# Query projection of the second batch by seven products instead of eight, in a fused cross-attention kernel

## The chip, the cores and the metric

The kernel runs on one core of a Trainium2 chip, in float32. The metric is the device time of one execution in microseconds. The kernel before takes 497.75 us (median of 3 runs, 497.58 to 497.92).

## The reference

Two batches of 2048 tokens (640 channels, 20 heads of 32) attend to 154 context rows, the first 77 and the last 77 each with a softmax of its own; both results are added, projected and added to the input.

```python
text, ip = ctx[:, :77], ctx[:, 77:]
q = split_heads(x @ Wq.T)                                   # (2, 20, 2048, 32)
out = attend(q, split_heads(text @ Wk.T), split_heads(text @ Wv.T)) \
    + attend(q, split_heads(ip @ Wk_ip.T), split_heads(ip @ Wv_ip.T))   # softmax(q k / sqrt(32)) v
return merge_heads(out) @ Wo.T + bo + x
```

## The kernel before

All matrices lie with the contracted dimension on the 128 partitions. The 640 channels are five chunks of 128, each four heads. One chunk of one batch is a step `q` (0 to 9, five for each batch); a step has two units `u` of 1024 tokens, and a unit has two blocks `h` of 512. For a block, `queries` (L198, matmul in L201) projects one chunk of queries: five matmuls of 128x128 weights by 512 tokens into one PSUM bank. `take_queries` (L209) reads the bank on ACT, scales it and puts it in one of five buffers `qT`. `scores` (L226, matmul in L233) multiplies 32-row heads by the keys. Then a group of the unit (three groups: 3, 3 and 2 tiles of 128 tokens; 24, 24 and 16 rows of heads) goes through the softmax: ACT copies the scores into `pb` (K, L245), DVE takes the maxima (M, L281 or L284), POOL subtracts them (S, L295), ACT takes exponentials (E, L301 or L269), DVE sums (D, L306) and inverts (I, L311), POOL normalises (N, L316), DVE transposes in 32x32 squares (T, L323). Groups in the table `DIRECT` skip K and S and read the bank; those in `BIASED` skip S and give the maxima to ACT as bias; in `SUMMED` ACT also makes the sums. When all six groups of a step are transposed, `attend` (L325, matmul in L332) multiplies by the values with 16 tiles of 32x32 in the array at a time, and ACT copies the result into `aT`. The projections of the keys and values (L142) and the output projection of the first batch (seven products for eight, L483 to L521, and L471 for the last chunk) fill PE between these. The second batch's output projection (L848, sums in L792 and L794) comes at the end.

A float32 matmul shows as two passes on PE in the profile: L201 has 200 matmuls and 400 passes.

The tokens lie in four resident blocks `xs` of 128x5x512 (1.28 MB). The first batch's four blocks are loaded once. For the second batch the blocks are loaded again for each unit and block, 20 times, into three of the places in turn (`place_of`, L179; `load_block`, L183); the fourth place holds sums of the output projection. The values are spread by small copies on SP's queue (`spread_v`, L154: eight for half a step).

The order of everything is the list `SCHEDULE`, a text that a planner wrote: `emit` (L632) goes through its words, and each engine does its instructions in that order. In a word the letter is the step, then come its numbers, and behind "@" the PSUM bank or half: `R0.10@1` are the scores of group 0 of unit 10, `q.10.0@3` the queries of unit 10, block 0, and `cq.10.0` their reading, `A.3@1` the attention of step 3, `m6.0` product 6 of the output projection, `LX` a load of a token block, `LQ` of query weights, `LO` of the output weights, `VS` a spread of values, `SF` and `SS` loads and stores of the output sums.

## Time and profile before

| | |
|---|---|
| median of 3 runs | 497.75 us |
| span of the profiled execution, first to last instruction | 496.7 us |
| PE busy | 490.3 us (99%) |
| DVE busy | 408.5 us (82%) |
| POOL busy | 362.5 us (73%) |
| ACT busy | 315.0 us (63%) |
| DMA, read and written | 54.94 and 10.49 MB, 132 GB/s over the span |

The profile is of one execution; its own time is its span of 496.7 us and about 1.0 us around it, by the median of the runs. Times are in microseconds unless marked ns. A row of the groups has the line, the engine, the operation, what it writes and reads, the shape, the count; then the busy time of all and the mean duration of one in ns; then the idle time of the engine just before them, and what ended it. PE's matmuls overlap each other, so the mean duration of one is longer than the distance from one to the next; the chain of waits, in order of time, gives that distance. PEld is the loading of weights, beside PE.

### The profile page before, as it was taken

The page shows a single profiled execution, that of the slowest core. Times are in us where ns is not written, and L with a number is a line of the kernel's source. Part 1 is how long each engine was busy: PE and PEld are TensorE (multiplying, and loading weights), DVE is VectorE, ACT ScalarE, POOL GpSimd, SP SyncE. Part 2 cuts the span into 40 slices and gives each one's busy share as a digit, 9 for nine tenths or more (in the row PEclk, how much of TensorE's full clock was granted, in tenths as well). Part 3 has the DMA queues.
Part 4 walks back from the last instruction along what each step waited for, and adds up shares of the span by engine and source line. Part 5 has one row for each costly group of instructions (what it writes and reads, how often), then busy time and mean ns, then how long its engine had stood idle before and what let it go on. Part 6 is the DMA issues. An engine that isn't in the chain of part 4 may idle for free.

```text
span 496.7 us, 10482 instructions
## 1 busy us (share of the span) xinstructions
PE 490.3 (99%) x4114; PEld 287.9 (58%) x4114; DVE 408.5 (82%) x412; ACT 315.0 (63%) x1021; POOL 362.5 (73%) x157
## 2 busy tenths in 40 slices
PE   8999999999999999999999999999999999999997
PEld 5676657657547556456647654755755675444442
DVE  0069989979979989969976896687999978898877
ACT  1165878978978778668999786587578966100000
POOL 0069978798888999989874858565899888284830
PEclk9999999999999999999999999999999999999999
DMA  8991440332360454886445177418525401420115
GB/s 259 356 246 40 132 120 1 106 93 69 92 213 3 132 178 132 274 273 237 158 152 191 58 244 210 133 57 246 174 69 171 127 23 43 149 84 1 43 73 223
DMA packets 67474, 69.38 MB, mean 140 GB/s; under 512 B 5473, under 2 KB 47201, under 8 KB 67425
## 3 DMA queue, kind: packets, MB, share of 16 engines
q1 hardware_dynamic: 66704, 68.00, 43.8%
q8 instruction: 32, 0.52, 0.5%
q10 hardware_dynamic: 720, 0.72, 0.4%
q14 instruction: 18, 0.14, 0.1%
HBM read 54.94 MB, written 10.49 MB: 132 GB/s over the span
## 4 chain that ended last, share of the span: by engine, by line
PE 92%; DMA 3%; SPq 1%; DVE 1%; POOL 1%; ACT 1%; issue 0%; POOLq 0%
PE bank L201 33%; PE bank L848 11%; PE bank L490 10%; PE bank L233 10%; PE bank L332 10%; PE bank L142 9%; PE bank L471 6%; PE bank L500 3%; DMA aT<-in_L_xattn_Wk_ip_dram 2%; DMA wq<-in_L_xattn_Wq_dram 2%; SPq L534 1%; POOL pb L316 1%; DVE den L306 0%; ACT pb L301 0%; SPq L132 0%
## 5 line engine op out<-in xcount | busy, mean ns | idle before, releaser
L316 POOL TENSOR_TENSOR pb<-pb,rden 128x1848 f32<-128x1848 f32 (+1 forms) x60 | 176.1, 2944 | 39.7 <-DVE rden L311 35.5
L201 PE MATMUL bank<-x,wq 128*128 128x512 f32 x400 | 180.4, 601 | 0.6 <-DMA x<-in_x_dram 0.5
L295 POOL TENSOR_TENSOR pb<-pb,mx 128x1848 f32<-128x1848 f32 (+1 forms) x38 | 119.3, 3152 | 51.8 <-DVE mx L281 51.5
L201 PEld LDWEIGHTS bank<-x,wq 128*128 128x128 f32 x400 | 74.1, 191 | 86.7 <-issue 80.8
L323 DVE STREAM_TRANSPOSE pb<-pb 128x1920 f32<-128x1920 f32 (+1 forms) x60 | 115.7, 1932 | 4.9 <-POOL pb L316 4.3
L281 DVE TENSOR_REDUCE mx<-pb 128x24 f32<-128x1848 f32 (+1 forms) x51 | 93.7, 1850 | 30.7 <-ACT pb L245 30.5
L245 ACT COPY pb<-bank 128x462 f32<-128x462 f32 (+1 forms) x204 | 87.2, 539 | 36.0 <-PE bank L233 35.4
L306 DVE TENSOR_REDUCE den<-pb 128x24 f32<-128x1848 f32 (+1 forms) x47 | 88.7, 1895 | 17.6 <-ACT pb L301 13.3
L301 ACT ACTIVATE pb<-pb 128x1848 f32<-128x1848 f32 (+1 forms) x38 | 64.2, 1696 | 17.8 <-POOL pb L295 17.5
L269 ACT ACTIVATE pb<-pb,mx 128x77 f32<-128x77 f32 x224 | 67.8, 364 | 0.3 <-DVE mx L281 0.2
L233 PEld LDWEIGHTS bank<-kT,qT 32*128 32x128 f32 x1280 | 45.4, 184 | 26.9 <-issue 15.6
L269 ACT ACTIVATE pb<-bank,mx 128x77 f32<-128x77 f32 x184 | 51.8, 386 | 9.3 <-DVE mx L284 9.3
L233 PE MATMUL bank<-kT,qT 32*128 32x154 f32 x1280 | 56.2, 305 | 0.3 <-ACT kT L559 0.3
L332 PE MATMUL bank<-pb,v 32*32 32x512 f32 x1600 | 55.2, 597 | 0.0
L142 PE MATMUL bank<-wo_ct,aT 128*128 128x154 f32 x320 | 45.6, 296 | 0.3 <-DMA aT<-in_L_xattn_Wk_ip_dram 0.3
L142 PEld LDWEIGHTS bank<-wo_ct,aT 128*128 128x128 f32 x320 | 42.9, 188 | 3.6 <-issue 2.2
L332 PEld LDWEIGHTS bank<-pb,v 32*32 32x32 f32 x1600 | 29.9, 103 | 22.8 <-issue 10.7
L211 ACT ACTIVATE qT<-bank 128x512 f32<-128x512 f32 x40 | 24.2, 619 | 22.1 <-PE bank L201 22.0
L471 PE MATMUL bank<-aT,wo_ct 128*128 128x512 f32 x80 | 36.1, 596 | 0.0
L269 ACT ACTIVATION_READ_ACCUMULATOR pb<-bank,mx 128x1 f32 x128 | 33.6, 267 | 0.0
L490 PE MATMUL bank<-aT,wo_ct 128*128 128x256 f32 x128 | 32.3, 385 | 0.0
L490 PEld LDWEIGHTS bank<-aT,wo_ct 128*128 128x128 f32 x128 | 23.7, 190 | 6.5 <-issue 3.0
(75 smaller groups left out, 434.4 us busy)
## 6 DMA issues: line engine op xcount, KB each, us to landing
x<-in_x_dram SPq DMA_DIRECT2D x20, 1280.0 KB, 6.7
out_dram<-acc SPq DMA_DIRECT2D x20, 256.0 KB, 2.3
x<-in_x_dram SPq DMA_DIRECT2D x18, 256.0 KB, 5.9
acc<-in_x_dram SPq DMA_DIRECT2D x16, 256.0 KB, 4.7
out_dram<-x SPq DMA_DIRECT2D x15, 256.0 KB, 2.0
v<-vS SPq DMA_DIRECT2D x160, 20.0 KB, 2.8
wq<-in_L_xattn_Wq_dram SPq DMA_DIRECT2D x9, 320.0 KB, 5.0
aT<-in_L_xattn_Wk_dram SPq DMA_DIRECT2D x5, 512.0 KB, 5.5
```

The source lines that it names most:

```text
L142: nc.tensor.matmul(keys_in(out), loaded[n][:, k, :], cT[:, k, :, t, :], start=(k == 0), stop=(k == NCC - 1))
L201: nc.tensor.matmul(pq, wqs[q % 3][:, k, :], xs[place_of(u, h)][:, k, :], start=(k == 0), stop=(k == NC - 1),)
L233: nc.tensor.matmul(ps[g][:, ts(t, 2 * L)], qTs[(u, h)][g * D : (g + 1) * D, ts(st, P)], kT[g * D : (g + 1) * D, c, b].rearrange("p t l -> ...
L245: nc.scalar.copy(keys_of(u, s)[:, :, g], ps[g][:, : n * 2 * L].rearrange("p (n l) -> p n l", n=n))
L269: nc.scalar.activation(row, row if ps is None else rows_in(ps[g], n)[:, t, x], AF.Exp, bias=maxs[(u, s)][:, *one], accum_out=None if den i ...
L281: nc.vector.tensor_reduce(mx, rows_of(u, s), AX.X, ALU.max, negate=negate)
L295: nc.gpsimd.tensor_tensor(rows_of(u, s), rows_of(u, s), maxs[(u, s)].unsqueeze(3).to_broadcast([P, n, 2, L]), ALU.subtract)
L306: nc.vector.tensor_reduce(den_of(u, s), rows_of(u, s), AX.X, ALU.add)
L316: nc.gpsimd.tensor_tensor(rows_of(u, s), rows_of(u, s), rdens[(u, s)].unsqueeze(3).to_broadcast([P, n, 2, L]), ALU.mult)
L323: nc.vector.transpose(p, p)
L332: nc.tensor.matmul(pa[r][g * D : (g + 1) * D, :], v4s[q % 2][rows, g, k, :], zones[rows, :, g, k, :], start=(k == 0), stop=(k == NK - 1),)
L490: nc.tensor.matmul(part, w_of[m][:, kp, op], t_of(m, b, i)[:, kp], start=(op == kp == 0 and m in (1, 2, 5)), stop=(op == 1 and kp == 1 and ...
```

## The change

For four of the second batch's five chunks (steps 5 and 6 are pair 0, steps 7 and 8 are pair 1) the queries of two chunks and one block of 512 tokens are made together. The two output chunks and the two halves of 256 tokens form a 2x2 block, and so do the four first input chunks (even and odd); seven products of 2x2 matmuls with sums of tokens and of weights take the place of eight, as the output projection already does. The fifth input chunk is added by four plain matmuls. Step 9 (units 18 and 19) and the first batch keep the old projection. The words are:

- `g.p.i.m` (`q_product`): product m of pair p and token block i on PE. Products 6, 7 and 4 go on in the bank of product 1, and 3 in that of 5.
- `t.p.i.m` (`take_q_product`): products 1, 5, 6 and 4 are read by ACT into a half of a query buffer, 2, 3 and 7 are added to or taken from it by DVE.
- `U.p.i.n.e` (`sum_x`): one of four sums of tokens, on POOL, or on DVE where e is d (the eight sums n = 2).
- `Z.p.n.e` (`sum_wq`): sums of query weights, on POOL, eight instructions for each pair.

Sums 2, 3 and 4 are written over the block that they are made from, so a block serves one pair only and is then loaded anew. There are 12 loads `LX` for 20, into two places in turn for three. The third place (`xs[2]`, `SPARE`) now holds two more query buffers, the first token sum and the weight sums; before, three of the second batch's blocks were still resident for the tail and the fourth was loaded into `acc` and `res`; now two are, and the third is loaded into the spare place ahead of the fourth, in `LA` (L809). The scale 1/sqrt(32) moves from the reading of the queries to that of the keys. `DIRECT` goes from 9 to 7 groups, `BIASED` from 13 to 16, `SUMMED` from 13 to 9, and the whole list is planned anew.

```diff
-        (11, 0), (13, 0), (13, 2), (14, 0), (14, 2), (15, 1), (15, 2), (16, 2), (18, 1),
+        (3, 2), (7, 1), (11, 0), (11, 2), (13, 0), (13, 2), (15, 1),
...
+    def first_of(u):
+        q, b, c, sub = step_of(u)
+        return u - SUB if b and c % 2 else u
 
     def place_of(u, h):
         _, b, _, sub = step_of(u)
-        return late.index((u, h)) % XROOM if b else sub * NH + h
+        return late.index((first_of(u), h)) % RING if b else sub * NH + h
...
+    spare = xs[SPARE].rearrange("p k t -> p (k t)")
+    q_more = [spare[:, ts(n, TB)] for n in range(2)]
+    x_first = spare[:, ds(2 * TB, TB)].rearrange("p (k t) -> p k t", k=2)
+    wq_room = spare[:, ds(3 * TB, 8 * P)].rearrange("p (k o) -> p k o", o=P)
...
-        nc.scalar.mul(qT, pq, SCALE)
-        qTs[(u, h)] = qT
+        nc.scalar.copy(new_q(u, h), pq)
...
+    def sum_x(p, i, n, eng):
+        x, y = {
+            1: lambda: (x_part(p, i, 0, 0), x_part(p, i, 0, 1)),
+            2: lambda: (x_sum(p, i, 1), x_part(p, i, 1, 1)),
+            3: lambda: (x_part(p, i, 0, 1), x_part(p, i, 1, 1)),
+            4: lambda: (x_sum(p, i, 2), x_part(p, i, 1, 0)),
+        }[n]()
+        eng.tensor_tensor(x_sum(p, i, n), x, y, ALU.add)
...
+        part = ps[:, :HT]
+        for kp in range(2):
+            nc.tensor.matmul(
+                part, w[:, kp], x[:, kp], start=(kp == 0 and m in (1, 2, 5)), stop=(kp == 1 and not fifth),
+                skip_group_check=True,
+            )
+        if fifth:
+            w5, h = fifth()
+            five = xs[place_of(*unit_of(p, i))][:, NC - 1, ts(h, HT)]
+            nc.tensor.matmul(part, w5, five, start=False, stop=True, skip_group_check=True)
...
+        t = (qTs[(u, h)] if (u, h) in qTs else new_q(u, h))[:, ts(half, HT)]
+        if m in (2, 3, 7):
+            nc.vector.tensor_tensor(t, t, ps[:, :HT], ALU.add if m == 2 else ALU.subtract)
+        elif half:
+            nc.scalar.mul(t, ps[:, :HT], -1.0)
+        else:
+            nc.scalar.copy(t, ps[:, :HT])
...
-        "R0.0@1 R1.0@0 K0.0 q.1.0@4 LK.5 K1.0 M0.0 M1.0 S0.0 R2.0@0 v.0.0@6 K2.0 cq.1.0 S1.0 M2.0 E0.0 v.0.1@0 LK.6 "
+        "LK.5 R2.0@0 K2.0 M2.0 R0.0@1 R1.0@0 K0.0 K1.0 E2.0 M0.0 S0.0 E0.0 q.1.0@4 M1.0 S1.0 D0.0 I0.0 LK.4 q.1.1@6 "
...
+            home[third] = xs[SPARE]
+            nc.sync.dma_start(
+                out=xs[SPARE], in_=xT[:, ds(S + third * TB, TB)].rearrange("(k p) t -> p k t", p=P)
+            )
```

What the new list does to three places of the program. The first is PE a few steps ahead of the attention of step 4, where the queries of units 10 and 11 are made. Before, three groups of queries stand together between scores (the last row of one unit's scores, the groups, the first row of the next):

```order
L233 MATMUL bank_7_74<-kT_79,qT_9_1_1528 128x154
L201 MATMUL bank_0_67<-x_1_83,wq_2_77 128x512 x5
L201 MATMUL bank_2_69<-x_2_84,wq_2_77 128x512 x5
L201 MATMUL bank_3_70<-x_0_82,wq_2_77 128x512 x5
L233 MATMUL bank_4_71<-kT_79,qT_10_0_1610 128x154
```

Now products of two token blocks are mixed there (blocks 1 and 2 of pair 0; `x_1` and `x_0` are the two places, `x_2` the spare one with the sums; L617 are the two matmuls of a product, L624 the fifth chunk, L143 a value projection):

```order
L617 MATMUL bank_5_69<-x_0_79,wq_2_74 128x256 x2
L143 MATMUL bank_0_64<-wo_ct_98,aT_83 128x154 x8
L617 MATMUL bank_4_68<-x_1_80,wq_0_72 128x256 x2
L624 MATMUL bank_4_68<-x_1_80,wq_0_72 128x256
L617 MATMUL bank_3_67<-x_0_79,wq_2_74 128x256 x2
L624 MATMUL bank_3_67<-x_0_79,wq_2_74 128x256
L617 MATMUL bank_1_65<-x_1_80,x_2_81 128x256 x2
L624 MATMUL bank_1_65<-x_1_80,x_2_81 128x256
L617 MATMUL bank_5_69<-x_0_79,x_2_81 128x256 x2
```

And a little later in the same list, products 5 and 3 of block 2 on bank 7, then product 7 on bank 5, between the scores of unit 10:

```order
L259 MATMUL bank_3_67<-kT_76,x_2_81 128x154
L617 MATMUL bank_7_71<-x_2_81 128x256 x2
L624 MATMUL bank_7_71<-x_0_79,x_2_81 128x256
L617 MATMUL bank_7_71<-x_0_79,x_2_81 128x256 x2
L624 MATMUL bank_7_71<-x_0_79,x_2_81 128x256
L617 MATMUL bank_5_69<-x_0_79,wq_0_72 128x256 x2
```

Groups of five wide matmuls have become pieces of two or three narrow ones, several banks are under way at once, and product 3 of block 2 follows product 5 on its bank with nothing between.

The second place is SP's queue at the second batch's first token blocks. Before (L186 loads a token block, L158 spreads values, L132 loads key or value weights, L192 query weights, L461 a part of the output sums):

```order
L186 DMA x_1_83<-in_x_dram 128x5x512
L158 DMA v4_1_81<-vS0_1_94 32x160 x8
L186 DMA x_2_84<-in_x_dram 128x5x512
L132 DMA aT_86<-in_L0_xattn_Wv_ip_dram 128x8x128
L461 DMA acc_87<-in_x_dram 128x2x256
L158 DMA v4_1_81<-vS1_95 32x160 x8
L186 DMA x_0_82<-in_x_dram 128x5x512
```

Now (L192 is the token block, L159 the spread, L133 the weights, L220 query weights, L165 the output weights):

```order
L192 DMA x_1_80<-in_x_dram 128x5x512
L133 DMA aT_83<-in_L0_xattn_Wv_ip_dram 128x8x128
L133 DMA aT_83<-in_L0_xattn_Wv_dram 128x8x128
L159 DMA v4_1_78<-vS1_97 32x160 x8
L192 DMA x_0_79<-in_x_dram 128x5x512
L220 DMA wq_1_73<-in_L0_xattn_Wq_dram 128x5x128
L165 DMA wo_ct_98<-in_L0_xattn_Wo_dram 128x5x640
L192 DMA x_1_80<-in_x_dram 128x5x512
```

The blocks alternate between two places, the third block stands behind eight spread copies, and the fourth behind the output weights.

The third place is DVE and POOL at units 8 and 9. DVE before (L281 maxima, L306 sums, L311 inverses, L323 transposes, L152 the squares of the values):

```order
L281 TENSOR_REDUCE mx_9_0_1679<-pb_89 128x24
L152 STREAM_TRANSPOSE vS0_0_93<-vT_91 128x160
L152 STREAM_TRANSPOSE vS1_95<-vT_91 128x160
L281 TENSOR_REDUCE mx_9_2_1727<-pb_89 128x16
L281 TENSOR_REDUCE mx_9_1_1745<-pb_89 128x24
```

DVE now (L308 maxima, L333 sums, L338 inverses, L570 a token sum, L633 a take of a product):

```order
L633 TENSOR_TENSOR x_2_81<-x_2_81,bank_3_67 128x256
L333 TENSOR_REDUCE den_8_2_1727<-pb_91 128x16
L338 RECIPROCAL rden_8_2_1729<-den_8_2_1727 128x16
L308 TENSOR_REDUCE mx_9_0_1733<-pb_91 128x24
L570 TENSOR_TENSOR x_1_80<-x_2_81,x_1_80 128x2x256
L308 TENSOR_REDUCE mx_9_2_1741<-pb_91 128x16
```

POOL now, at the same place (L322 subtracts, L343 normalises, L570 a token sum):

```order
L322 TENSOR_TENSOR pb_91<-pb_91,mx_8_1_1648 128x12x154
L570 TENSOR_TENSOR x_2_81<-x_1_80 128x512
L343 TENSOR_TENSOR pb_91<-pb_91,rden_8_0_1653 128x12x154
L570 TENSOR_TENSOR x_1_80<-x_1_80 128x2x256
L322 TENSOR_TENSOR pb_91<-pb_91,mx_9_0_1733 128x12x154
L343 TENSOR_TENSOR pb_91<-pb_91,rden_8_2_1729 128x8x154
```

Takes and token sums stand between the softmax operations on both engines; DVE's token sum (sum 2 of block 1) reads what POOL's first one (sum 1) wrote, while POOL goes on with its list.

More of the change, by code (lines that the diff above doesn't have):

```diff
@@ L92 @@
     aT = const.tile([P, (NC + 1) * NHB, TB], F32, name="aT")
+    q_slots = [const.tile([P, TB], F32, name=f"qs_{n}") for n in range(QS)]
     acc = const.tile([P, NC - 1, TB], F32, name="acc")
@@ L188, in load_block, with new_q, used_q @@
         )
+    spare = xs[SPARE].rearrange("p k t -> p (k t)")
+    q_more = [spare[:, ts(n, TB)] for n in range(2)]
+    x_first = spare[:, ds(2 * TB, TB)].rearrange("p (k t) -> p k t", k=2)
+    wq_room = spare[:, ds(3 * TB, 8 * P)].rearrange("p (k o) -> p k o", o=P)
+    q_uses, q_idle, q_late = {}, list(q_slots), list(q_more)
+    def new_q(u, h):
+        if u >= NU // 2 and q_late:
+            q_idle[:0] = q_late
+            q_late.clear()
+        t = q_idle.pop(0)
+        qTs[(u, h)], q_uses[(u, h)] = t, NT // NH
+        return t
+    def used_q(u, h):
+        q_uses[(u, h)] -= 1
+        if not q_uses[(u, h)]:
+            q_idle.append(qTs[(u, h)])
     def load_wq(q):
@@ L809, in finish @@
         elif k == "LA":
-            for u, h in late[-XROOM:]:
+            for u, h in late[-RING:]:
                 home[step_of(u)[3] * NH + h] = xs[place_of(u, h)]
-            (fourth,) = set(range(NHB)) - set(home)
+            third, fourth = sorted(set(range(NHB)) - set(home))
+            home[third] = xs[SPARE]
+            nc.sync.dma_start(
+                out=xs[SPARE], in_=xT[:, ds(S + third * TB, TB)].rearrange("(k p) t -> p k t", p=P)
+            )
             nc.sync.dma_start(
```

71 lines of the change are left out of this document (63 added, 8 removed), and 131 rows, old and new, of the table SCHEDULE.

## The prediction

> **What bounds the kernel now.** I read the page first: who is busy, and what the last chain is made of.
>
> ```profile
> span 496.7 us, 10482 instructions
> PE 490.3 (99%) x4114; PEld 287.9 (58%) x4114; DVE 408.5 (82%) x412; ACT 315.0 (63%) x1021; POOL 362.5 (73%) x157
> PE 92%; DMA 3%; SPq 1%; DVE 1%; POOL 1%; ACT 1%; issue 0%; POOLq 0%
> L201 PE MATMUL bank<-x,wq 128*128 128x512 f32 x400 | 180.4, 601 | 0.6 <-DMA x<-in_x_dram 0.5
> ```
>
> PE is busy 99% of the span, and 92% of the last chain is PE. The costliest group is the projection of the queries (L201): 400 passes, two for each of its 200 matmuls. So an edit is worth what it takes off PE's own row, less any wait that it opens there. "Busy" need not mean well spaced, so I then read the chain of waits in order of time, between 180 and 262 us.
>
> ```profile
> 224.07 0.86 PE bank L490 x4
> ...
> 225.36 4.29 PE bank L471 x10
> ...
> 234.19 0.74 PE bank L233 x16
> 234.92 4.49 PE bank L201 x10
> 239.41 1.00 PE bank L233 x24
> ```
>
> This gives the prices. A 512-column pass follows the last one after 429 ns (4.29 for 10), a 256-column pass after 215 ns (0.86 for 4). The scores (L233) work on 32 rows: 8 more of their passes cost 0.26 (1.00 less 0.74), so 16 are worth 0.52, and a visit costs 0.22 beyond its work. The ten passes between two such visits cost 0.20 more than ten that follow other 128-row work (4.49 against 4.29). A visit to 32-row work thus costs 0.42 us in turns.
>
> Who could take PE's place? I read the windows for the two fullest stretches between attentions.
>
> ```profile
> 211.60:254.60 43.00, 42.92 (x386) 24.80 (x382) 39.04 (x35) 36.69 (x131) 37.31 (x17) 1.00 0.59 194
> 346.00:388.70 42.70, 42.70 (x397) 26.19 (x400) 40.37 (x38) 31.78 (x101) 38.84 (x17) 1.00 0.45 140
> ```
>
> The columns are PE, PEld, DVE, ACT and POOL, then PE's granted clock. In the second stretch DVE is 95% busy and POOL 91%, while PE misses nothing, at full clock. The softmax engines are close behind PE without holding it.
>
> **The change, part by part.** Durations are from this one execution, whose span is 496.7; the median of the runs is 497.75, 1.0 us more, and I add the sum to the median.
>
> *The products.* Sixteen of the forty query groups go: 160 passes of 429 ns, 68.6 us. In their place stand eight token blocks (two pairs of channel blocks, four blocks each) of seven products. A product has two matmuls over the four first input chunks, and four of the seven have one more for the fifth: 18 matmuls, 36 passes of 256 columns. That is 288 passes of 215 ns, 61.9 us. PE gains 6.7 us, a tenth of the part: the fifth chunk is not spared.
>
> *Turns.* In the new order PE visits 32-row work 54 times, before 50 (scores and attentions in a row counted as one). Four times 0.42 is 1.7 us back. Gain so far 5.0.
>
> *Joined products.* Products 6, 7 and 4 are added in the bank of product 1, and 3 in that of 5, once ACT or DVE has read it. These are 32 new places where PE waits for a reader. The output projection of the first batch has 16 such places now, and the groups by form show what PE lost there.
>
> ```profile
> L490 PE MATMUL bank<-aT,x 128*128 128x256 f32 x64 | 16.4, 388 | 0.4 <-DVE acc L515 0.2
> L490 PE MATMUL bank<-x 128*128 128x256 f32 x32 | 8.6, 391 | 0.1
> L359 ACT COPY aT<-bank 128x256 f32<-128x256 f32 x40 | 11.4, 404 | 12.1 <-POOL pb L828 10.8 <-PE bank L332 1.3
> ```
>
> 0.5 us over 16 places is 0.03 each; 31 new ones cost 0.9. The thirty-second has no cover at all: in the order shown with the change, products 5 and 3 of the third block stand directly behind each other on bank 7. PE waits there for its own drain (a pass lasts 388 and is followed after 215, so about 0.17) and an ACT reading of 256 columns (0.40): 0.6 us. The bounds for all are 0 and 32 times 0.6, 19 us, if none had cover; but the other 31 have 0.7 us or more of other passes between, most over 2, so I stay near the low end. Gain left: 3.5.
>
> *Takes, sums, softmax tables.* These rows price them.
>
> ```profile
> L316 POOL TENSOR_TENSOR pb<-pb,rden 128x1848 f32<-128x1848 f32 x40 | 131.3, 3288 | 24.8 <-DVE rden L311 22.7 <-ACT aT L355 1.1 <-ACT pb L245 0.6
> L295 POOL TENSOR_TENSOR pb<-pb,mx 128x1848 f32<-128x1848 f32 x33 | 108.3, 3289 | 51.8 <-DVE mx L281 51.5
> L295 POOL TENSOR_TENSOR pb<-pb,mx 128x1232 f32<-128x1232 f32 x5 | 11.3, 2253 | 0.0
> L431 POOL TENSOR_TENSOR aT<-aT 128x512 f32<-128x512 f32 x8 | 10.2, 1278 | 0.1
> L401 POOL TENSOR_TENSOR x<-wo_ct 128x256 f32<-128x256 f32 x1 | 0.7, 736 | 0.0
> L323 DVE STREAM_TRANSPOSE pb<-pb 128x1920 f32<-128x1920 f32 x40 | 86.3, 2160 | 3.7 <-POOL pb L316 3.2
> L281 DVE TENSOR_REDUCE mx<-pb 128x24 f32<-128x1848 f32 x35 | 71.5, 2051 | 28.4 <-ACT pb L245 28.3
> L515 DVE SCALAR_TENSOR_TENSOR acc<-bank,bo_sb,acc 128x256 f32<-128x256 f32 x32 | 13.7, 468 | 7.0 <-PE bank L500 7.0
> L834 DVE TENSOR_TENSOR pb<-aT 128x1024 f32<-128x1024 f32 x7 | 8.3, 1221 | 1.7 <-PE bank L332 1.5 <-ACT aT L359 0.2
> L306 DVE TENSOR_REDUCE den<-pb 128x16 f32<-128x1232 f32 x12 | 16.9, 1412 | 3.6 <-ACT pb L269 3.6
> ```
>
> POOL gets 24 token sums of 1.28 (30.7) and, for each pair, six weight operations of 0.74 and two that I estimate at 0.5 (10.9 in all). The new tables leave 26 large and 11 small subtractions for 33 and 5: 9.3 less. POOL goes from 362.5 to some 395, 80% of the new span. DVE gets 24 takes (0.47 each at most, 11.2), 8 token sums of half an L834 (0.61, 4.9) and four more small sums of exponentials (5.6): some 430, 87%. ACT loses 16 readings of 512 columns for 32 of 256; it is busy 63%.
>
> I cost this at nothing on PE, and the cover is the lead that DVE and POOL have. I priced DVE's instructions in the new order up to the last transpose that each attention needs, and PE's up to that attention, both by rows such as these (neighbours on DVE overlap by 0.08). DVE starts at 27.4 us, as its first row shows:
>
> ```profile
> 27.42 4.06 DVE L281 TENSOR_REDUCE mx<-pb 128x24 f32<-128x1848 f32 x2 [26.42 <-ACT pb L245]
> ```
>
> By that count DVE's work leaves 7 us before the first attention, 10 to 15 before the next three, 16 to 25 later; in the old order it is 4, 6, and up to 46. POOL has 9 and more. So the lead is thinner late and thicker early, and nowhere under what it is now at its thinnest. The bounds are 0 and rival B.
>
> *Two resident blocks for three.* Twelve loads of 1.28 MB replace twenty, and one more moves to the tail. What matters is PE's work between the last reading of a slot and the first use of its next block. By the prices above it is 9.3 us at least now; in the new order four loads have 10.2, 8.0, 7.9 and 11.0. A load takes, by the view of its line, and a group of eight spread copies that stands ahead of one on SP's queue, by SP's timeline:
>
> ```profile
> DMA to landing us min/median/max: 6.1/6.7/10.6
> ```
> ```profile
> 161.20 5.95 SPq L158 DMA_DIRECT2D v<-vS  x8
> ```
>
> At the median all four fit. The second, with 8.0, is issued right behind the output weights (1.6 MB), and I give it 0.5 us; bounds 0 and rival C. Behind a late load SP's queue holds spread copies and stores, for which nobody waits at once. Gain left: 3.0.
>
> *The ends of the program.* At the front the third group of scores goes ahead of the first two; the matmuls are the same, at 0. In the tail the third block is loaded ahead of the last accumulator.
>
> ```profile
> 424.56 0.38 SPq L813 DMA_DIRECT2D acc<-in_x_dram  x1
> ```
> ```profile
> 438.77 0.74 DVE L792 SCALAR_TENSOR_TENSOR acc<-acc,bo_sb,bank 128x512 f32<-128x512 f32 x1
> 439.43 0.74 DVE L792 SCALAR_TENSOR_TENSOR x<-x,bo_sb,bank 128x512 f32<-128x512 f32 x1
> ```
>
> There are 14.2 us between issue and use now. Two blocks in a row take about the slowest landing, 10.6; the use comes earlier in the new order, so I put 0 to 2 and take 0. Moving the scale from queries to keys changes no instruction's size.
>
> Sum: 6.7 less 1.7, 0.9, 0.6 and 0.5 is 3.0 gained: 497.75 - 3.0 = 494.7.
>
> **The rivals.** *A, no new waits.* All joins and loads are covered: 497.75 - 5.0 = 492.7. For it: PE lost 0.5 us in 16 joins. Against it: the join without cover.
>
> *B, DVE and POOL hold each other up.* Both get operations with two inputs from SBUF. The timelines of the tail, DVE first, then POOL:
>
> ```profile
> 436.11 0.28 DVE L828 TENSOR_TENSOR pb<-pb,wo_ct 128x128 f32<-128x128 f32 x1
> ...
> 472.73 1.50 DVE L828 TENSOR_TENSOR pb<-pb,wo_ct 128x128 f32<-128x128 f32 x1
> ```
> ```profile
> 469.41 4.66 POOL L834 TENSOR_TENSOR aT<-aT 128x1024 f32<-128x1024 f32 x2
> ```
>
> The same DVE sum took 0.28 with POOL idle and 1.50 when it met a running POOL sum: it ended at 474.23, just behind POOL's end at 474.07. The eight DVE token sums stand, in the new order, between softmax steps while POOL has operations of 3.29. Meeting one halfway costs 1.6 each, 13 us of DVE in all, and POOL is pushed back by 0.61 each, 4.9. If 5 of these 18 us reach PE, the time is 492.7 + 5 = 497.7. For it: between attentions 4 and 5 POOL has 42.1 us of work in the new list (two subtractions, six normalisations, nine sums of 1.28, the weights) against 38 of PE. Against it: the leads, which such a loss doesn't use up.
>
> The Trainium skill says this as a rule (SBUF — State Buffer, section "SBUF: two separate sides"): the port pair that these two engines share is an exclusive lock, and an operation of DVE with two SBUF inputs and one of GpSimd keep each other out for a whole instruction. The trace agrees (1.50 against 0.28).
>
> *C, late blocks, slower.* The four tight loads land like the slowest, 10.6, the first of them behind a group of spread copies that can't start before the attention ahead is done: late by 3.8 (5.95 + 10.6, against 10.2 and two products, 2.6), 2.6, 2.7 and 0. PE issues in order and stands still: 492.7 + 9.1 = 501.8. It decides once the sum passes 6 us. For it: the 1.6 MB load. Against it: the median landing.
>
> *D, the passes don't come at half price.* At 238 ns (68.6 over 288) the products gain nothing, and the turns remain: 499.4. For it, in the groups by form:
>
> ```profile
> L490 PEld LDWEIGHTS bank<-aT,wo_ct 128*128 128x128 f32 x128 | 23.7, 190 | 6.5 <-issue 3.0 <-DVE acc L521 0.3 <-ACT pb L269 0.2
> ```
>
> A weight load of 190 leaves only 25 of the 215. Against it: L490 has the same shapes, and keeps 215.
>
> **How the numbers follow.** Forecast 0.52 (its own range 493.2 to 496.5); A 0.20; B 0.14, from 496 to 499; C 0.08; D 0.06. A measurement of this kernel tells 0.2%, 1.0 us, from no change. Faster, under 496.75: the forecast but 0.02, A and 0.06 of B, 0.76. Within 0.2%: those 0.02, half of B (0.07) and half of D (0.03), 0.12. Slower: C, the other half of D and the last of B, 0.12. The range 492.0 to 498.0 takes in A and most of B, and leaves out C, D and B's end, under 0.2.
>
> **What would show it.** Right: on the chain, query lines of 103 us for 240 passes and 62 for 288; PE 98% busy; 1 to 2 us of idle before the new products, most of it at the third block's product 3. A: less than 0.5 there. B: DVE token sums (0.61 alone) of 1.5 to 3, and PE waiting for DVE or POOL before scores and attentions from the third attention on. C: PE waiting for x. The forecast is wrong if PE's idle time in the middle of the program grows by more than 3.5 us, or if a 256-column pass comes further apart than 220 ns.

## The result: 515.6 us for 497.6, slower by 3.7%

| | before | after |
|---|---|---|
| median of five runs, us | 497.58 (497.00 to 497.92) | 515.61 (514.77 to 517.58) |
| ratio, 95% interval | | 1.0366 [1.0348, 1.0384] |
| span of the profiled execution | 496.7 | 514.8 |
| start to first attention | 69.8 | 69.2 |
| first to tenth attention | 353.8 | 356.7 |
| tenth attention to PE's last product | 69.4 | 85.0 |

The forecast was 494.7. Of the 18.1 us that the span grew, 15.6 lie behind the tenth attention. To the output projection at the end the change gives only a new order of its words and the load of one more block; its sums, with their engines, its products and its readings are the old ones. In that order 12 weight sums and 2 token sums that stood ahead of the tenth attention stand behind it, and one of each goes the other way.

The page of the changed kernel: the span, the busy times, the clock that PE was granted in 40 slices, and the last chain.

```profile
span 514.8 us, 10868 instructions
PE 496.8 (97%) x4242; PEld 317.0 (62%) x4242; DVE 442.6 (86%) x442; ACT 327.3 (64%) x1052; POOL 400.5 (78%) x196
PEclk9999999999999999999999999999999899889989
PE 75%; DVE 18%; ACT 4%; issue 2%; ACTq 0%; DVEq 0%
```

DVE's share of the chain went from 1% to 18%, PE is busy 97% for 99%, and the clock falls to 8 tenths in four late slices; it had fallen nowhere before. The windows of the two parts, for the kernel before and then for the changed one (length, then PE, PEld, DVE, ACT, POOL, PE's clock, DMA):

```profile
69.80:423.60 353.80, 353.28 (x3399) 215.57 (x3398) 308.94 (x291) 278.91 (x944) 291.01 (x120) 1.00 0.44 138
423.60:493.00 69.40, 69.39 (x309) 30.69 (x308) 59.14 (x92) 2.31 (x8) 32.76 (x20) 1.00 0.24 86
```
```profile
69.20:425.90 356.70, 353.30 (x3527) 241.78 (x3526) 332.68 (x320) 284.08 (x928) 325.27 (x152) 1.00 0.35 105
425.90:510.90 85.00, 75.74 (x309) 32.64 (x308) 72.21 (x95) 2.31 (x8) 43.92 (x29) 0.92 0.23 85
```

In the last part PE runs the same 309 instructions. It stands idle for 9.3 us (85.00 less 75.74), and the instructions themselves take 6.3 us more, at a mean clock of 0.92. PE's waits in the changed kernel say for whom (total, times, longest):

```profile
PE bank L984 <- DVE x L926: 5.5, 2, 3.4
PE bank L984 <- DVE x L924: 3.8, 1, 3.8
PE bank L517 <- DVE acc L542: 2.0, 1, 2.0
```

L924 and L926 are DVE's readings of the banks, which themselves take what they always took (0.74 and 0.68). What stood ahead of them in DVE's queue did not: these are the sums of weights and tokens for the output projection. The timelines of DVE, POOL and PE around the first of these waits:

```profile
439.38 2.43 DVE L964 TENSOR_TENSOR pb<-pb,wo_ct 128x128 f32<-128x128 f32 x1
...
444.36 3.21 DVE L970 TENSOR_TENSOR pb<-aT 128x1024 f32<-128x1024 f32 x1
447.50 0.73 DVE L924 SCALAR_TENSOR_TENSOR x<-x,bo_sb,bank 128x512 f32<-128x512 f32 x1
```
```profile
438.34 3.32 POOL L970 TENSOR_TENSOR aT<-aT 128x1024 f32<-128x1024 f32 x1
...
444.15 2.34 POOL L970 TENSOR_TENSOR pb<-aT,pb 128x1024 f32<-128x1024 f32 x1
```
```profile
443.49 1.02 PE L984 MATMUL bank<-x,wo_ct 128*128 128x512 f32 x2
448.29 2.07 PE L984 MATMUL bank<-pb 128*128 128x512 f32 x2 [3.78 <-DVE x L924]
450.15 1.91 PE L984 MATMUL bank<-pb,wo_ct 128*128 128x512 f32 x2
451.86 1.06 PE L984 MATMUL bank<-aT,wo_ct 128*128 128x512 f32 x1
```

A weight sum of 128 columns, 0.28 us elsewhere, took 2.43 and ended at 441.81, 0.15 behind POOL's token sum (441.66). A token sum of DVE, 1.21 elsewhere, took 3.21: POOL had started one 0.21 us earlier. PE came at 444.5 to a bank that DVE could read only at 447.5, and waited 3.8 us. Then its passes came 853 ns apart for 429: two last 2.07 and 1.91 in the rows, for 1.02. Ahead of the second wait DVE has two weight sums of 2.43 (at 467.4 and 469.8), ahead of the third a token sum of 3.40 (at 486.0). A *meeting* is meant below where such a sum of DVE and an operation of POOL are under way at once and one of them ends late. The groups by form show it in sum, for the changed kernel and then before, both behind the tenth attention:

```profile
L970 DVE TENSOR_TENSOR pb<-aT 128x1024 f32<-128x1024 f32 x7 | 11.2, 1629 | 2.3 <-ACT aT L386 2.3
L964 DVE TENSOR_TENSOR pb<-pb,wo_ct 128x128 f32<-128x128 f32 x10 | 8.0, 798 | 0.1
```
```profile
L834 DVE TENSOR_TENSOR pb<-aT 128x1024 f32<-128x1024 f32 x7 | 8.3, 1221 | 1.7 <-PE bank L332 1.5 <-ACT aT L359 0.2
L828 DVE TENSOR_TENSOR pb<-pb,wo_ct 128x128 f32<-128x128 f32 x10 | 4.1, 429 | 0.0
```

Added over all DVE sums of that part, each against the usual duration of its form, the meetings cost DVE 14.0 us in 14 operations, before 1.9 in 4 (counted from just ahead of the tenth attention). In the old order DVE does most of its sums from 424 to 437 us, where POOL has three of 0.5 to 0.8 us, and POOL does its own from 436.5 on. The new order mixes the two.

One meeting stands ahead of the tenth attention. DVE, POOL and PE:

```profile
399.51 3.35 DVE L964 TENSOR_TENSOR pb<-pb,wo_ct 128x128 f32<-128x128 f32 x1
402.78 1.50 DVE L350 STREAM_TRANSPOSE pb<-pb 128x1280 f32<-128x1280 f32 x1
404.21 0.83 DVE L542 SCALAR_TENSOR_TENSOR acc<-bank,bo_sb,acc 128x256 f32<-128x256 f32 x2
```
```profile
399.42 3.29 POOL L322 TENSOR_TENSOR pb<-pb,mx 128x1848 f32<-128x1848 f32 x1 [0.51 <-DVE mx L308]
```
```profile
405.09 1.58 PE L517 MATMUL bank<-aT,x 128*128 128x256 f32 x4 [1.99 <-DVE acc L542]
```

A weight sum (V.P, its second instruction) met a softmax subtraction 0.09 us after that began, a transpose and a reading came 3.1 us late behind it, and PE waited 2.0.

### The profile page after: what moved, and what is told of

It is laid out like the page before. It is cut to its first block, busy times and chain, and to the rows that moved or that the text cites. A ratio compares the mean times of both kernels' runs of the same rounds, so it can differ in the third digit from the quotient of the medians.

```text
span 514.8 us, 10868 instructions
## 1 busy us (share of the span) xinstructions
PE 496.8 (97%) x4242; PEld 317.0 (62%) x4242; DVE 442.6 (86%) x442; ACT 327.3 (64%) x1052; POOL 400.5 (78%) x196
## 4 chain that ended last, share of the span: by engine, by line
PE 75%; DVE 18%; ACT 4%; issue 2%; ACTq 0%; DVEq 0%
PE bank L229 18%; PE bank L259 9%; PE bank L359 8%; PE bank L984 8%; PE bank L517 8%; PE bank L143 8%; PE bank L617 7%; DVE pb L350 4%; PE bank L498 3%; DVE mx L308 3%; DVE den L333 2%; DVE pb L970 2%; PE bank L527 2%; PE bank L624 2%; ACT pb L296 2%
## 5 line engine op out<-in xcount | busy, mean ns | idle before, releaser
L343 POOL TENSOR_TENSOR pb<-pb,rden 128x1848 f32<-128x1848 f32 (+1 forms) x60 | 176.1, 2946 | 23.2 <-DVE rden L338 20.1
L322 POOL TENSOR_TENSOR pb<-pb,mx 128x1848 f32<-128x1848 f32 (+1 forms) x37 | 110.4, 2991 | 42.7 <-DVE mx L308 42.4
L308 DVE TENSOR_REDUCE mx<-pb 128x24 f32<-128x1848 f32 (+1 forms) x53 | 97.5, 1849 | 28.9 <-ACT pb L272 28.8
L229 PE MATMUL bank<-x,wq 128*128 128x512 f32 x240 | 108.2, 602 | 0.1
L333 DVE TENSOR_REDUCE den<-pb 128x24 f32<-128x1848 f32 (+1 forms) x51 | 94.4, 1853 | 15.3 <-ACT pb L328 11.0
L296 ACT ACTIVATE pb<-pb,mx 128x77 f32<-128x77 f32 x336 | 94.8, 366 | 2.8 <-DVE mx L308 2.8
L229 PEld LDWEIGHTS bank<-x,wq 128*128 128x128 f32 x240 | 44.6, 191 | 52.6 <-issue 49.4
L328 ACT ACTIVATE pb<-pb 128x1848 f32<-128x1848 f32 (+1 forms) x37 | 60.0, 1624 | 18.2 <-POOL pb L322 18.2
L259 PEld LDWEIGHTS bank<-kT,qs 32*128 32x128 f32 x1024 | 37.8, 184 | 18.6 <-issue 12.0
L259 PE MATMUL bank<-kT,qs 32*128 32x154 f32 x1024 | 48.3, 308 | 0.4 <-ACT kT L674 0.3
L143 PEld LDWEIGHTS bank<-wo_ct,aT 128*128 128x128 f32 x320 | 43.2, 188 | 4.1 <-issue 3.0
L143 PE MATMUL bank<-wo_ct,aT 128*128 128x154 f32 x320 | 45.5, 295 | 0.1
L296 ACT ACTIVATE pb<-bank,mx 128x77 f32<-128x77 f32 x144 | 38.7, 398 | 0.8 <-DVE mx L311 0.8
L570 POOL TENSOR_TENSOR x<-x 128x512 f32<-128x512 f32 x24 | 31.9, 1334 | 2.4 <-DMA x<-in_x_dram 1.2
L617 PE MATMUL bank<-x,wq 128*128 128x256 f32 x128 | 33.4, 387 | 0.1
L926 DVE TENSOR_TENSOR x<-x,bank 128x512 f32<-128x512 f32 x36 | 23.4, 681 | 6.7 <-PE bank L984 6.4
```

The lines of the kernel that those rows point to most:

```text
L143: nc.tensor.matmul(keys_in(out), loaded[n][:, k, :], cT[:, k, :, t, :], start=(k == 0), stop=(k == NCC - 1))
L229: nc.tensor.matmul(pq, wqs[q % 3][:, k, :], xs[place_of(u, h)][:, k, :], start=(k == 0), stop=(k == NC - 1),)
L259: nc.tensor.matmul(ps[g][:, ts(t, 2 * L)], qTs[(u, h)][g * D : (g + 1) * D, ts(st, P)], kT[g * D : (g + 1) * D, c, b].rearrange("p t l -> ...
L296: nc.scalar.activation(row, row if ps is None else rows_in(ps[g], n)[:, t, x], AF.Exp, bias=maxs[(u, s)][:, *one], accum_out=None if den i ...
L308: nc.vector.tensor_reduce(mx, rows_of(u, s), AX.X, ALU.max, negate=negate)
L322: nc.gpsimd.tensor_tensor(rows_of(u, s), rows_of(u, s), maxs[(u, s)].unsqueeze(3).to_broadcast([P, n, 2, L]), ALU.subtract)
```

## The experiments

The theory was then: DVE operations with two inputs from SBUF and POOL operations keep each other out for a whole instruction (rival B's mechanism), but the costly place is the tail, where the readings that PE waits for stand in the same queue. Rivals: the new tail leaves its sums too little lead, lock or not (the order theory); the third token block, now loaded in the tail, comes late (the load theory).

**e1_old_tail and e2_new_tail** exchange the order of the tail between the two kernels (words as in the list: V weight sum, X token sum, F product, Y reading, the last letter d for DVE and p for POOL):

```
e1, in after.py:
- A.9@0 SS.3.4 V.Q.0.d X.A.p@1 V.X.0.p V.X.1.p V.X.2.p F31.1@6 ...
+ A.9@0 V.C.0.p V.S.0.d V.N.0.d LA V.U.0.d X.G.d@0 X.C.d@3 ...
e2, in before.py: the same the other way round
```

> The changed kernel with the order of the kernel before for the tail alone: all weight sums (V) and token sums (X) of the last product block stand where the kernel before has them, and everything behind the tenth attention is in its order; all before that, and the loads, are as changed. In the changed kernel the stretch from the tenth attention to PE's last product is 85.0 us (69.4 before), the stage ahead of it 38.4 (35.0). The lock theory (DVE sums with two SBUF inputs are held by running POOL operations, PE stands for them 2 to 4 us each and then runs at half clock) and the order theory (the new order leaves these sums too little lead, lock or not): the last stretch goes back to 69 to 73, the sum V.P.1 falls elsewhere, and the time is 497 to 502. The load theory (the third token block, now loaded in the tail, comes late): the stretch stays above 80 and the time above 510.

Measured: 506.68 us, 1.0191 [1.0174, 1.0207] against before. The last stretch is 71.4 us, as the lock and the order theory have it, and DVE loses 1.5 us to meetings there, in 2 operations. The time is worse than forecast because the stage ahead of the tenth attention went to 42.6 us. By the timelines, POOL has two token sums (2.4 us each) and small weight sums of the old order ahead of its last softmax steps there, and a meeting comes on top, DVE first, then the last of six small POOL sums in a row:

```profile
425.81 2.35 DVE L964 TENSOR_TENSOR pb<-wo_ct 128x128 f32<-128x128 f32 x1
```
```profile
427.54 0.47 POOL L964 TENSOR_TENSOR pb<-wo_ct 128x128 f32<-128x128 f32 x1
```

DVE's sum began while the first of the six was running (425.48 to 425.95) and ended 0.15 us behind the last (428.01): POOL's operations followed each other without a gap, and DVE did not get in between. The transpose that the attention waits for stood behind it. PE waited 7.0 us at that attention, and the attention itself then took 7.58 us for 5.52.

> The kernel before with the changed kernel's order for the tail alone (weight sums, token sums and everything behind the tenth attention). No query product, no token sum in the middle and no late third block is in it. Lock and order theory: its last stretch, 69.4 us in the kernel before, becomes 76 to 86, and the time 504 to 514 for 497.6. By the lock theory it hangs on which operations meet to within a microsecond, so the number may be anywhere in that range; by the order theory it is 15 longer again. Load theory: no change, 496 to 499.

Measured: 512.23 us, 1.0292 [1.0270, 1.0313]. The order of the tail alone costs the kernel before 14.7 us. Its window:

```profile
423.30:507.40 84.10, 74.85 (x309) 31.99 (x308) 71.58 (x95) 2.31 (x8) 43.62 (x28) 0.94 0.19 71
```

84.1 us, with no token sum in the middle and no late third block in the program: the load theory falls.

**e3_one_input** keeps the order and takes the second input of DVE's sums away, which leaves the second term out of the result:

```
+ alone = lambda eng, out, a: eng is nc.vector and (eng.tensor_reduce(out, a.unsqueeze(len(a.shape)), AX.X, ALU.add), True)[1]
- eng.tensor_tensor(out, out if j else weight(a), weight(b), o2)
+ alone(eng, out, out if j else weight(a)) or eng.tensor_tensor(out, out if j else weight(a), weight(b), o2)
  (in the same way the two other sums of V and X)
```

> The changed kernel in its own order, with DVE's weight and token sums of the last block (33 of them) replaced by a reduction of the same size over one input, which leaves the second term out, so that DVE has no operation with two SBUF inputs from 399 us on. Lock theory: these take 0.3 us (128 columns) and 1.1 to 1.4 (1024) wherever POOL is, no wait of PE above 1 us is left behind the tenth attention, no passes at half clock; the last stretch is 69 to 73 us and the stage ahead of it 35 to 36: 497 to 502 in all. Order theory and load theory: the stretch stays above 80, the time above 510.

Measured: 497.65 us, 1.0004 [0.9995, 1.0014] against before, 18.0 less than the changed kernel. Its window behind the tenth attention, and two groups there:

```profile
422.30:491.70 69.40, 69.40 (x309) 30.64 (x308) 58.37 (x95) 2.31 (x8) 37.53 (x29) 1.00 0.29 105
```
```profile
L933 DVE TENSOR_REDUCE pb<-aT 128x1024 f32<-128x1024 f32 x7 | 8.3, 1211 | 3.4 <-ACT aT L386 3.4
...
L933 DVE TENSOR_REDUCE pb<-pb 128x128 f32<-128x128 f32 x12 | 3.3, 279 | 0.1
```

The order, the queues and the lengths are the changed kernel's; only the second input is gone, and the stretch takes 69.4 us, as before, with PE busy throughout at full clock. The order theory without a lock falls. Without the second input DVE need not wait for it to be ready either, but that is not the gain: behind the changed kernel's tenth attention DVE waited for PE (9.6 us) and ACT (2.3) alone, never for a sum of POOL.

**e4_vp_on_pool** moves V.P:

```
- V.P.0.d S1.19 V.P.1.d
+ V.P.0.p S1.19 V.P.1.p
```

> The changed kernel with one weight sum (V.P, two instructions of 128 columns) on POOL in place of DVE. On DVE its second instruction took 3.35 us for 0.28, beside a POOL subtraction of 3.29, and PE waited 2.05 us at 402.8 behind it. Lock theory: that wait is gone and the stage between the ninth and tenth attention goes from 38.4 to 35 to 36 us; the time falls by 3 if the tail's meetings stay as they are, which it does not promise: 509 to 515. If that wait came from something else, the stage stays at 38.

Measured: 512.68 us, 1.0308 [1.0286, 1.0330]. The wait ahead of 405.1 in the row above is gone, the stage takes 35.2 us for 38.4, and the last stretch stays at 85.0.

**e5_one_input_mid** is e3 with the same edit in the middle:

```
- eng.tensor_tensor(x_sum(p, i, n), x, y, ALU.add)
+ eng.tensor_reduce(x_sum(p, i, n), x.unsqueeze(3), AX.X, ALU.add) if eng is nc.vector else eng.tensor_tensor(...)
```

> The kernel e3 (DVE's sums of the last block reduced over one input) with DVE's eight token sums in the middle (128 x 512) made one-input reductions as well, which leaves their second term out. No operation of DVE with two SBUF inputs is left but the joins from the banks. In e3 two of the eight took 1.7 us for 0.68, and from the first to the tenth attention it needs 352.9 us. If the lock costs PE something in the middle (the place that rival B named), this stretch falls by 1 to 3 and the time to 495 to 496.5; if the leads there cover it, it stays at 352.5 to 353 and the time at 497.2 to 497.8.

Measured: 497.02 us, 0.9984 [0.9975, 0.9993]. From the first to the tenth attention the profile has 351.7 us for e3's 352.8 (352.9 in the text on record): the lock costs PE some 1.1 us at the place that rival B named. The times can't confirm so little: e8, measured beside it with the meetings in the middle still there, has 497.01. The profile of e4 agrees by chance. There the fourth of these token sums keeps its second input but met nothing and took 0.68 us (1.62 in e3), and the stages behind the fourth and the fifth attention took 42.6 and 40.7 us, for 43.1 and 41.1 in e3 and 42.6 and 40.5 in e5.

**e6_lock_order** keeps the arithmetic, has V.P on POOL as e4, and gives the words behind the tenth attention another order, found by a small replay that charges the meetings; the engine letters of 13 weight sums there change (of 33; the text on record counts 42, too many):

```
- A.9@0 SS.3.4 V.Q.0.d X.A.p@1 V.X.0.p V.X.1.p V.X.2.p F31.1@6 SS.3.0 V.E.0.d V.N.0.d V.N.1.d X.C.d@3 ...
+ A.9@0 V.F.0.p V.A.0.d V.E.0.d X.C.d@3 V.Q.0.d V.B.0.d V.L.0.d V.X.0.d V.T.0.d SS.3.4 SS.3.0 V.T.1.d ...
```

> The changed kernel, whole and with the reference's arithmetic, with V.P on POOL as in e4 and the words behind the tenth attention in an order found by a replay that charges each DVE operation with two SBUF inputs and each POOL operation for the other's time where they meet (13 of the 42 weight sums left there change engine, products and readings move too). The replay, with durations from the traces, gives the changed kernel 79.5 us there with waits of 3.6 and 3.6 us, the kernel before 69.0 and this order 69.0, with under 2 us of lock. Lock theory: the last stretch measures 69 to 71 us, DVE loses under 3 us to meetings there (14.0 in the changed kernel), no wait of PE above 1 us, and the time is 496.5 to 498.5. If the last stretch costs more for another reason (loads, banks, half clock by itself), it stays above 75.

Measured: 498.02 us, 1.0007 [0.9998, 1.0016]. 17.6 us of the 18.0 are back, DVE loses 1.3 us to meetings in the tail (3 operations), and no wait of PE there is left above 0.3:

```profile
422.70:492.40 69.70, 69.32 (x309) 30.81 (x308) 58.65 (x94) 2.31 (x8) 39.98 (x29) 1.00 0.29 104
```

So the loss is settled. What stays open is the gain: without any of it the changed kernel is level with the one before, where the forecast had 3 us. Five experiments went after that, two of them on e3 and three on e6.

**e7_lock_order_cover** puts cover in front of the product that the prediction called uncovered:

```
- g.0.2.5@7 t.0.2.5 T0.9 g.0.2.3 LX.11.1 U.0.3.1.p K0.10 VS.4.0 g.0.2.7
+ g.0.2.5@7 t.0.2.5 T0.9 g.0.2.7 g.0.2.3 LX.11.1 U.0.3.1.p K0.10 VS.4.0
```

> As e6, and in the middle product 7 of the third token block goes ahead of its product 3, so that product 3 no longer stands directly behind product 5 on the same bank; it waited there 0.86 us for ACT (the prediction put 0.6). If that wait is as read, this is faster than e6 by 0.6 to 0.9 us: 495.7 to 497.8, and the gap at 209 us is gone. If PE only waits for something else a little later, the time equals e6's.

Measured: 498.34 us, 1.0012 [1.0003, 1.0021], no better than e6. The changed kernel's row at product 3, then e7's at product 7, which now stands there:

```profile
210.43 0.92 PE L617 MATMUL bank<-x,x 128*128 128x256 f32 x3 [0.69 <-ACT qs L635]
```
```profile
211.04 1.10 PE L617 MATMUL bank<-x,wq 128*128 128x256 f32 x4 [0.52 <-ACT qs L635]
```

Product 7 waits for ACT's reading of product 6, which is as late as that of product 5: ACT does three readings from 210.25 to 211.16. The gap was read as a missing cover; it is a late ACT, and cover of 0.86 us does not reach.

**e8_short_exp** is e3 with ACT's exponentials ahead of the longer of two slow visits to the scores made short, by leaving out the subtraction of the maxima and the sums:

```
+ few = (u, s) == (11, 0)
+ if few: nc.scalar.activation(keys_of(u, s)[:, :, g], ps[g][:, : n * 2 * L].rearrange(...), AF.Exp)
- for t in range(n):
+ for t in range(0 if few else n):
```

> The kernel e3 with ACT's 24 exponentials of 77 columns for one group of scores (group 0 of step 11, 7.2 us of ACT from 233 to 240 us) done as four of 462 columns without bias and a copy, about 2.5 us, which is not the softmax. In e3 the visit of 56 score passes behind them (239.7 us) takes 3.74 us, by the row price of 16 for 0.52 and 24 for 1.00 about 2.2, and the visit of 24 before it (230.4) 2.17 for 1.00. If these visits wait for ACT to read the banks, the second falls to 2.2 to 2.5 and the first stays at 2.2, and the time is 1.3 to 1.6 below e3: 496.0 to 496.5. If they wait for DVE or POOL, both stay and the time is that of e3, 497.6.

Measured: 497.01 us, 0.9988 [0.9979, 0.9997]; but the visit of 56 stays at 3.74, the one before at 2.17, and the stretch between first and tenth attention at 352.8. ACT and then PE of e8:

```profile
234.85 1.88 ACT L296 ACTIVATE pb<-bank 128x462 f32<-128x462 f32 x4
240.65 3.17 ACT L272 COPY pb<-bank 128x462 f32<-128x462 f32 x8 [3.92 <-PE bank L259]
```
```profile
239.56 0.54 PE L259 MATMUL bank<-kT,qs 32*128 32x154 f32 x8
239.93 0.70 PE L259 MATMUL bank<-kT,x 32*128 32x154 f32 x16
240.68 0.81 PE L259 MATMUL bank<-kT,qs 32*128 32x154 f32 x16
241.31 2.07 PE L259 MATMUL bank<-kT,x 32*128 32x154 f32 x16
```

ACT now stands idle 3.9 us and waits for PE. The last 16 passes take 2.07 for the 0.70 of the first 16: they fill the banks that the first 24 had just filled, and ACT needs four readings of some 0.4 us in between, however early it is free. So this wait is not that of a busy ACT; by these rows it comes from the order of the visits.

**e9_score_turn** moves the group that stands between the two away:

```
- R1.11@0 K1.11 R2.12@1 N0.10 Z.1.6.p T0.10 I1.10 G5.0 R2.11@0 I0.11 M2.11 K2.12 N2.10 M1.11 g.1.0.1@5 g.1.0.2@4
+ R1.11@0 K1.11 g.1.0.1@5 g.1.0.2@4 N0.10 Z.1.6.p T0.10 I1.10 G5.0 R2.11@0 I0.11 M2.11 N2.10 M1.11
- U.1.0.4.p g.1.0.3
+ U.1.0.4.p R2.12@0 K2.12 g.1.0.3
```

> As e6, and one group of scores (group 2 of step 12) leaves the visit of 56 passes at 239.7 us for a visit of its own at 257 us, on the other half of the banks; two products stand in its place. In e3, e6 and e8 that visit takes 3.74 us whatever ACT does before it, since group 1 of step 11 fills four banks, ACT reads them (four readings of 0.4 us), and group 2 of the same step is to fill the same four right behind. If this turn on the banks is the wait: the two visits take 1.0 each, the separate visit 0.74, the stretch from the fourth to the fifth attention falls by 1.0 to 1.2, and the time is 496.6 to 497.4 for e6's 498.0. If PE is held by the softmax engines as such, the waits show up again ahead of the next attention, and the time is e6's.

Measured: 499.72 us, 1.0037 [1.0023, 1.0051], slower than e6. The visit itself lost its wait (1.00 and 0.74). But two waits of 0.5 and 1.1 us appear behind it, at 249 and 252 us, both for DVE's readings of the banks, the added visit takes its turn too, and the stage takes 42.4 us for 41.1. The stage ahead of it takes 43.6 for 43.0; its DVE token sum met POOL for 2.05 us, 1.48 in e6.

**e11_fewer_sums** is e3 without 16 of POOL's token sums. It asks whether POOL holds those stages (it is busy 99% of one):

```
- sum_x(x, y, int(args[2]), ...)
+ args[2] in "34" or sum_x(x, y, int(args[2]), ...)
```

> The kernel e3 with 16 of POOL's 24 token sums (numbers 3 and 4 of each token block, 1.28 us each) left out, so that products 7 and 4 use raw tokens. In e3 POOL is busy 40.94 of 41.10 us between the fifth and the sixth attention and 40.98 of 43.10 in the stage before it. Those two stages take 84.2 us; by the list, with passes and visits to 32-row work at their row prices and no waits, 78.7. POOL theory (the token sums make POOL the bound there, and PE's waits ahead of two visits and at product 3 are where that shows): the two stages fall to 79 to 81.5 and the time to 494 to 496. Bank theory (two visits wait for banks that were filled just before, whatever POOL does): the visit of 56 passes stays at 3.74, the two stages lose under 1 us, and the time is 496.5 to 497.6.

Measured: 496.98 us, 0.9985 [0.9975, 0.9995]. POOL's busy time in the two stages falls from 81.9 to 72.5 us, and they take 83.7 for 84.2; the visit of 56 stays at 3.74. POOL is full there, and not the bound.

**e12_two_sums_moved** is e6 with the two token sums of the middle that met POOL put on POOL (`U.0.3.2.d` and `U.1.1.2.d` become `.p`).

> As e6, with the two token sums of DVE that met a POOL operation in the middle (second sum of the fourth block of pair 0 and of the second block of pair 1, 1.5 and 1.7 us for 0.68) put on POOL, whole and with the reference's arithmetic. e5 took the lock out of the middle by leaving work out, and the stretch from the first to the tenth attention fell by 1.2 us against e3. If those two meetings are that loss and POOL is not the bound there (e11), the stretch falls from e6's 353.1 to 351.9 to 352.4 and the time to 496.7 to 497.4. If POOL's 2.6 us more cost as much as the meetings, it stays at 353 or above and the time at 498.

Measured: 500.28 us, 1.0051 [1.0037, 1.0065], a miss. At the second sum the stage gains 0.6 us as in e5. The first now stands behind a normalisation and another sum on POOL; product 6 waited 1.9 us for it, and five passes later PE's passes came at half the rate: the stage is 46.6 us for 43.0. That is the profile of the longest of six executions (501.81 us, mean clock 0.997). Three others, at 0.999 and more, took 499.2 to 499.8, still more than e6's 498.0: a meeting of 0.8 us (1.48 for 0.68) was cheaper than the queue, half clock or not.

**e10_idle_dve** is e3 with DVE kept busy by useless reductions ahead of three readings (`B.3` before Y6.0.10, `B.6` before Y7.0.21, `B.14` before Y7.1.30).

> The kernel e3, in which DVE meets no lock, with DVE kept busy by reductions of 512 columns that nobody reads, ahead of three of its bank readings in the tail: 3, 6 and 14 of them (0.6 us each), so that PE waits by the replay about 1.5, 2.4 and 6 us. It tells whether the half clock after PE's waits belongs to the lock or to any wait. If to any wait of some length: behind the longer ones the passes come 853 ns apart for about 3.5 us, as in the changed kernel, and each costs 1.3 to 2.3 us beyond the wait; the time is e3's 497.6 plus 10 to 16. If to the lock: the passes stay at 429, and the time is 497.6 plus the waits, about 10.

Measured, in one execution: 512.53 us, the last stretch 84.0. PE behind the three waits:

```profile
442.93 1.12 PE L989 MATMUL bank<-pb 128*128 128x512 f32 x2 [1.48 <-DVE x L928]
```
```profile
456.36 1.13 PE L989 MATMUL bank<-aT,pb 128*128 128x512 f32 x2 [2.86 <-DVE x L930]
...
489.17 4.53 PE L989 MATMUL bank<-pb 128*128 128x512 f32 x6 [7.46 <-DVE acc L930]
```

Without any lock a wait of 7.5 us is followed by half clock (six passes last 4.53; at 429 apart they would last 2.7); waits of 1.5 and 2.9 are not. So the half clock does not need the lock.

## Why the prediction was wrong, point by point

- **Products.** Right in mechanism and size. Behind one another the 256-column passes come 215 to 216 ns apart, so 288 of them are 62.1 us for 160 passes of 429 (68.6). Rival D falls.
- **Turns and joins.** Visits and joins were put at 3.2 us (1.7, 0.9 and 0.6). In e5, by the spacing of PE's passes per line against before, they come to about 2.3 (query passes 70.8 less, products 67.1 more, output products and the rest 0.8 less, scores 2.4 more of which 2.1 are the waits of the next point: a gain of 2.1 in all, where 6.5 would be the passes alone). The one join in 32 that waits visibly is the one named, 0.7 to 0.9 for 0.6, though for a late ACT.
- **Visits that turn on the banks** were not in the sum. In e3 two visits to the scores wait 1.2 and 1.5 us, in e5 0.6 and 1.5, where their banks were filled just before and are still to be read; that is most of what the middle falls short of the forecast. e8 and e11 show that neither ACT's nor POOL's load is behind the larger one, and e9 that taking it away lets other waits up. What holds this stage after that stays open.
- **Two resident blocks.** PE waited for none; the 0.5 for the fourth load did not show, and rival C falls. POOL alone waited 1.2 us for a late block.
- **Takes, sums, softmax tables at nothing, covered by the leads, and "The ends of the program" at nothing:** this is the step that failed. The count of leads stopped at the last attention, and for the tail the prediction priced one load and no order, although the difference of the two orders was in front of it. Behind the last attention DVE has no lead: every reading of a bank stands in the same queue as the sums and is waited for at once. There the new order mixes DVE's sums with POOL's; 14.0 us of meetings became 9.3 us of idle PE and 6.3 of passes at half clock. In the middle PE's idle time grew by 2.9 us (356.70 less 353.30, for 353.80 less 353.28), so the prediction's own sign of being wrong, more than 3.5 there, did not show; it named none for the tail.
- **Rival B** had the mechanism, the price of a meeting (1.50 for 0.28 in the row shown) and the wrong place: eight token sums in the middle, 18 us of DVE and POOL, 5 on PE. In the changed kernel two of the eight took 1.82 and 1.75 us and a third 1.02, for 0.68, and by e5 they cost PE some 1.1. It had the rows of the tail in hand and used them for a price only. The Trainium skill (SBUF — State Buffer, section "SBUF: two separate sides") says that the shared port pair is an exclusive lock, that a DVE operation with two SBUF inputs takes part in it, and that whoever starts first keeps it for the whole instruction. The trace agrees to 0.15 us (441.81 against POOL's 441.66), and e3 agrees on the other side: with one input the same columns take 0.28 beside a running POOL. In e1 DVE was kept out by six POOL operations in a row, not by one.
- **The range** took PE's waits as their own cost. Behind four of four waits of 3.4 us and more in the tails of the changed kernel and of e2 the passes come some 853 ns apart until 3.3 to 6.1 us after PE's restart, and that costs 1.6 to 3.1 us on top of each wait.

Together, in us between first attention and last product: tail lock 15.6 (85.0 against e3's 69.4), V.P 3.2 to 3.6 (38.4 against 35.2 in e4 and 34.8 in e3), lock in the middle 1.1, and a gain of 2.1 for the forecast's 3.0 once all three are gone (e5). 15.6 + 3.6 + 1.1 - 2.1 is 18.2; the two windows differ by 18.5. Of the gain of 2.1 the medians show less: e5 takes 497.02 for 497.73, 0.7 us. The profile of the kernel before is of a long execution, since every run with both numbers takes 1.8 us more than its span, and 496.7 and 1.8 are 498.5 for a median of 497.6. The stretch ahead of the first attention is in no window of this sum and varies from 68.4 to 70.2 us over the profiles of all kernels, so where the rest of the gain goes is not shown.

## What to carry to other kernels

Where two engines exclude each other, a change of order is a change of cost: compare the two orders at the places where their shared operations lie close, above all behind the last point that has a lead. A list that lets DVE and POOL take turns in long stretches is worth keeping, and a planner that moves them needs the meeting in its replay; with that, the same sums and products, 15 of the weight sums on the other engine, cost 17.6 us less here. And a wait of PE is dearer than its length once the clock falls behind it.

## What the runs showed of the hardware

**The half clock after a wait** has no clean threshold in these profiles. PE of the changed kernel behind its second and third wait in the tail:

```profile
474.24 2.05 PE L984 MATMUL bank<-x,pb 128*128 128x512 f32 x2 [3.42 <-DVE x L926]
...
490.08 1.24 PE L984 MATMUL bank<-pb 128*128 128x512 f32 x2 [2.06 <-DVE x L926]
491.11 1.91 PE L984 MATMUL bank<-aT,pb 128*128 128x512 f32 x2
```

Behind the waits of 3.8 and 3.4 us it came at once (two passes last 2.05 for 1.02). Behind 2.0 (from 403.1 to 405.1) it came two passes later, with eight 256-column passes some 427 ns apart; behind 2.1 (from 488.0 to 490.1) two passes later as well, and so in e4; behind 1.9 in e12 five passes later. In e2 it did not come behind a wait of the same 2.06 us at the same place of the same order, nor behind 1.5 and 2.9 in e10. The five executions of the changed kernel have mean clocks of 0.983 to 0.990, so the falls differ from one execution to the next. The Trainium skill (TensorE: Matmul & The Clock Gate, section "Part 1: The HAM clock gate") says that PE falls to half clock after an idle window of about 3.4 us. By that rule the waits of about 2 us would be free; here four of five were not, and each of the four cost 1.7 to 1.9 us more.

**Both sides of a meeting lose.** POOL's token sums of 2.35 took 3.2 to 3.3 where a DVE sum had begun first, and its small sums 1.4 for 0.45; 6.8 us in the tail of the changed kernel; PE's waits there name DVE alone, not POOL.
